# A two-layer graph network on one core: new start and end of the instruction order, adjacency casts behind the weights, row sums of the first attention on TensorE

## The chip, the cores and the metric

One core of one Trainium2 chip runs the kernel in one launch. The metric is the device time of that core in microseconds. The engines named below are TensorE (PE; its weight loads are shown apart as PEld), VectorE (DVE), ScalarE (ACT), GpSimd (POOL) and SyncE (SP). SP computes nothing here; it issues transfers.

## The reference

32 graphs of 512 nodes with 256 features each go through two layers. Heads are 8 with 32 features. Shortened:

```python
def layer0(x, adj):                       # transformer layer
    allowed = (adj > 0) | (adj.T > 0) | eye
    q, k, v = split(x @ Wqkv.T + bqkv)
    attn = softmax(where(allowed, (q / sqrt(32)) @ k.T, -inf))
    x = layernorm(x + (attn @ v) @ Wo.T + bo) * g1 + b1n
    return layernorm(x + relu(x @ W1.T + b1) @ W2.T + b2) * g2 + b2n
def layer1(x, adj):                       # attention alone, mask adj != 0
    return (softmax(where(adj != 0, q @ k.T / sqrt(32), -inf)) @ v) @ Wo.T + bo
x = layernorm(x + layer0(x, adj))
x = layernorm(x + layer1(x, adj))
```

All of it is float32; adj is a 512 x 512 int32 matrix for each graph.

## The kernel before

Each graph is an object (`class Graph`, L218) whose methods issue one step of the work each. All steps are written out by hand in one order: `opening` (L630, the first five graphs until the pattern repeats), `period` (L1534, called for k = 1 to 26, with five neighbouring graphs a to e in different stages), and `closing` (L1837, the last five graphs). Every engine executes its own instructions in exactly that order, and a step waits for its inputs and for the buffer that it writes. Which of several buffers a tile gets is written out too, as strings of digits (`slots`, L166): "d" for the three PSUM banks of the dense products, "p" for the eight buffers of attention weights, and so on.

The steps that matter here, with P = 128, NQ = 4 blocks of nodes, ND = 2 blocks of features:

- `load` (L310) brings x of a graph to SBUF by SP. `constants(a, b)` (L337) issues the loads of entries a to b-1 of a list of weights by SP: 0 is Wqkv (768 KB), 1 to 3 its biases, 4 and 5 Wo and bo of layer 0, 6 and 7 W1 (1 MB) and b1, 8 and 9 W2 and b2, 10 to 13 norm weights, 14 to 21 layer 1, 22 a second copy of b2 as a column.
- `cast` (L313) turns adj into bf16 by a DMA from POOL's queue (HBM to HBM). `entries` (L319) loads the result, `entry(i)` (L322) loads a block of it transposed, both from SP. `masks(i)` (L325) makes the two masks of it on DVE.
- `transpose` and `transpose_out` make xT of the first graph on PE and ACT (tile psT). For later graphs `flip`, `sort` (transfers by SP) and `join` (ACT) do that.
- `query_key` (psQK), `value` (psV), `project` (psO), `hidden` (psH) and `mlp` (psF) are products through `dense` (L159), which issues them with 128 columns of weights (`wide=True`) or four times with 32.
- `scores(layer, k)` (L441) writes 4 heads x 512 scores of a block of 128 keys to the one tile s in PSUM; `exp` (L456) takes it to a p buffer on ACT; `masked` (L459) multiplies p by the mask on DVE; `product` (L463) multiplies p with v on PE into the one tile acc, and `context` copies that out on ACT. Eight values of k make an attention.
- The row sums of p are needed to divide. `pair` (L479) adds one p to another by an accumulating DMA of POOL's queue, `fold` (L483) adds two on DVE. For heads 0 to 3 `halve` (L505) and `spread` (L510) go on by DMA and `blocks` and `reduce` end it on DVE; for heads 4 to 7 `sums` (L486) adds over partitions on PE, 4 products with a matrix of ones (tile psR). Where `direct` (L244) is true, which holds for the last graph's layer 1 only, there is no folding: `sums` runs 16 products for each half of the heads.
- `once(i)` (L342) computes constants on PE: 0 and 1 bv @ Wo (4 matmul instructions each), and 2 the product of W1 with the column b2, whose moving side has one column, 32 matmul instructions. The result is subtracted from b1 in `once_out`.
- `store` (L627) writes the result of a graph by one transfer of SP.

A float32 product appears as two matmul instructions in the trace. The order of the old opening, until the second graph's first product, is:

```python
a.load(); a.cast(); a.constants(0, 4); a.transpose(0, 1); a.transpose_out(0, 1); b.flip(1); b.sort(1, 0, 0)
a.entries(); a.transpose(0, 0); a.transpose_out(0, 0); a.query_key(0, 0, 0, None, wide=True); a.entry(3)
a.entry(1); a.query_key_out(0, 0, 0, None); b.cast(); a.query_key(0, 1, 0, None, wide=True)
a.query_key_out(0, 1, 0, None); a.entry(0); a.entry(2); a.masks(0); a.scores(0, 3); a.exp(0, 3)
a.scores(0, 2); a.exp(0, 2); a.query_key(0, 1, 1, None); b.flip(0); a.scores(0, 0); a.exp(0, 0); a.masks(1)
a.masks(2); a.value(0, 0); a.value_out(0, 0); a.scores(0, 1); b.sort(1, 0, 1); a.exp(0, 1)
a.query_key(0, 0, 1, None); a.query_key_out(0, 1, 1, None); a.query_key_out(0, 0, 1, None); a.value(0, 1)
a.masked(0, 0); b.sort(1, 1, 0); a.value_out(0, 1); a.masked(0, 1); a.scores(0, 5); a.exp(0, 5)
a.constants(22, 23); a.product(0, 0); a.pair(0, 0); a.constants(4, 6); a.once(0); b.sort(0, 1, 0)
a.product(0, 1); b.sort(0, 0, 0); a.masked(0, 2); a.constants(10, 12); a.masked(0, 3); b.sort(1, 1, 1)
a.scores(0, 4); a.exp(0, 4); a.masked(0, 4); a.scores(0, 6); b.sort(0, 1, 1); b.join(0, 1); a.exp(0, 6)
a.product(0, 2); a.scores(0, 7); a.exp(0, 7); a.masked(0, 7); a.product(0, 3); a.context(0, 0); b.join(1, 0)
b.sort(0, 0, 1); a.pair(0, 2); a.fold(0, 2, 2, 0); a.product(0, 4); a.once_out(0); a.bias(1); b.join(0, 0)
b.entry(0); b.value(0, 0); b.join(1, 1); b.query_key(0, 1, 0, None)
...
```

The old closing ends with:

```python
e.product(1, 7); e.guard(0, 0, 1); e.widen(1, 1); e.context(1, 1); e.divide(1, 1); e.project(1, 0)
e.add(4, 1); e.add(4, 0); e.stats(4, 1); e.guard(0, 1, 1); e.guard(1, 0, 0); e.project(1, 1); e.stats(4, 0)
e.aggregate(4, 0); e.aggregate(4, 1); e.add(4, 3); e.add(4, 2); e.stats(4, 3); e.stats(4, 2)
e.aggregate(4, 3); e.aggregate(4, 2); e.root(4, 0, 2); e.offset(4, 0, 2); e.norm(4, 1); e.norm(4, 0)
d.guard(1, 0, 0); e.root(4, 2, 4); e.guard(1, 1, 1); e.offset(4, 2, 4); e.norm(4, 3); e.norm(4, 2)
e.store()
```

Of the kernel before, what the change touches and what calls it, by code (L numbers as in the profile page):

```python
# [14 lines left out]
ALU = mybir.AluOpType  # L15
# [12 lines left out]
def kernel(ctx: ExitStack, tc: tile.TileContext, t: dict, out: bass.AP):  # L28
# [12 lines left out]
    nc = tc.nc  # L41
    x, adj = t["x"], t["adj"]
    B, N, D = x.shape
    P = 128
# [106 lines left out]
    def plain(pools: ExitStack):  # L151
# [7 lines left out]
        def dense(out, lhsT, rhs, start, stop, wide):  # L159

            for at in (slice(0, P),) if wide else [slice(j * HD, (j + 1) * HD) for j in range(HPC)]:
# [3 lines left out]

        slots = {  # L166
            "d": iter(
                "012012021021122121012012010210210210201012102021121021012012012012102102102102102020120122021201212101120120212010"
                + "120121212010121212012012120120021212102101010212101010210210102102201010" * 13
                + "102120201210021021010210102102102021201021010210202101201201210210212102102102121021021021021021202102120120"  # L170
            ),
            "p": iter(
                "012345673267415013405762302764517064153205732146706431520752136450436217051726431"
                + "036472501257436206435710271536470436152075216435036421705172436106437250125736420436571027156437036415207521436506432170517236410436725012576432036457102715436706431520752136450436217051726431" * 2
                + "03642750175246370435612072516437063124563452170"
            ),
            "y": iter(
                "01231023012301231023100113201320232301321023020231201302"
                + "303021031230232301321023020231201302" * 8
                + "3202132031200210203102312020021032101230"  # L180
            ),
            "z": iter(
                "011010010110"
                + "01101001" * 13
                + "011010010101"
            ),
            "st": iter(
                "01230123012301230132103210321032102310231023"
                + "12032103210321031230213021302130" * 13
                + "1203123012031023031203210312031203123210320132013021"  # L190
            ),
            "r": iter(
                "0123331303"
                + "23301003" * 13
                + "11100313021131"
# [7 lines left out]
                "01100110"  # L203
                + "0110" * 13
                + "0110"
            ),
            "total": iter(
                "01110"
                + "0110" * 13
                + "0101001"  # L210
# [7 lines left out]
        class Graph:  # L218
# [25 lines left out]
            def direct(self, layer):  # L244

                return (self.b, layer) == (B - 1, 1)
# [62 lines left out]

            def load(self):  # L310
                nc.sync.dma_start(out=self.x, in_=x[self.b].rearrange("(c p) d -> p c d", p=P))

            def cast(self):  # L313
                nc.gpsimd.dma_start(
                    out=self.code.rearrange("(p c) k -> p (c k)", p=P),
                    in_=adj[self.b].rearrange("(p c) k -> p (c k)", p=P),
                )

# [18 lines left out]
            def constants(self, a, b):  # L337

                for dst, src in resident[a:b]:
                    nc.sync.dma_start(out=dst, in_=src)  # L340

            def once(self, i):  # L342
# [8 lines left out]
                ps = self.bank("B", (i,), [NF])  # L351
                for f in range(NF):
                    for c in range(ND):
                        nc.tensor.matmul(  # L354
                            ps[:, f : f + 1],
                            w1[:, c, f * P : (f + 1) * P],
                            b2_c[:, c : c + 1],
# [4 lines left out]
            def once_out(self, i):  # L362
# [4 lines left out]
                nc.vector.tensor_tensor(b1, b1, self.bank("B", (i,), [NF]), ALU.subtract)  # L367
# [259 lines left out]
            def store(self):  # L627
                nc.sync.dma_start(out=out[self.b].rearrange("(c p) d -> p c d", p=P), in_=self.x2)

        def opening(a, b, c, d, e):  # L630

            a.load()
            a.cast()
            a.constants(0, 4)
            a.transpose(0, 1)
            a.transpose_out(0, 1)
            b.flip(1)
            b.sort(1, 0, 0)
            a.entries()
            a.transpose(0, 0)  # L640
            a.transpose_out(0, 0)
            a.query_key(0, 0, 0, None, wide=True)
            a.entry(3)
            a.entry(1)
            a.query_key_out(0, 0, 0, None)
            b.cast()
            a.query_key(0, 1, 0, None, wide=True)
            a.query_key_out(0, 1, 0, None)
            a.entry(0)
            a.entry(2)  # L650
            a.masks(0)
            a.scores(0, 3)
            a.exp(0, 3)
            a.scores(0, 2)
            a.exp(0, 2)
            a.query_key(0, 1, 1, None)
            b.flip(0)
            a.scores(0, 0)
            a.exp(0, 0)
            a.masks(1)  # L660
            a.masks(2)
            a.value(0, 0)
            a.value_out(0, 0)
            a.scores(0, 1)
            b.sort(1, 0, 1)
            a.exp(0, 1)
            a.query_key(0, 0, 1, None)
            a.query_key_out(0, 1, 1, None)
            a.query_key_out(0, 0, 1, None)
            a.value(0, 1)  # L670
            a.masked(0, 0)
            b.sort(1, 1, 0)
            a.value_out(0, 1)
            a.masked(0, 1)
            a.scores(0, 5)
            a.exp(0, 5)
            a.constants(22, 23)
            a.product(0, 0)
            a.pair(0, 0)
            a.constants(4, 6)  # L680
            a.once(0)
            b.sort(0, 1, 0)
            a.product(0, 1)
            b.sort(0, 0, 0)
            a.masked(0, 2)
            a.constants(10, 12)
            a.masked(0, 3)
            b.sort(1, 1, 1)
            a.scores(0, 4)
            a.exp(0, 4)  # L690
            a.masked(0, 4)
            a.scores(0, 6)
            b.sort(0, 1, 1)
            b.join(0, 1)
            a.exp(0, 6)
            a.product(0, 2)
            a.scores(0, 7)
            a.exp(0, 7)
            a.masked(0, 7)
            a.product(0, 3)  # L700
            a.context(0, 0)
            b.join(1, 0)
            b.sort(0, 0, 1)
            a.pair(0, 2)
            a.fold(0, 2, 2, 0)
            a.product(0, 4)
            a.once_out(0)
            a.bias(1)
            b.join(0, 0)
            b.entry(0)  # L710
            b.value(0, 0)
            b.join(1, 1)
            b.query_key(0, 1, 0, None)
            a.halve(0, 0, P // 2)
            b.query_key(0, 0, 0, None)
            b.query_key_out(0, 0, 0, None)
            b.query_key_out(0, 1, 0, None)
            b.query_key(0, 1, 1, None)
            b.scores(0, 0)
            b.value(0, 1)  # L720
            a.halve(0, 0, P // 4)
            b.exp(0, 0)
            a.masked(0, 5)
            a.product(0, 5)
            b.value_out(0, 1)
            b.query_key(0, 0, 1, None)
            a.masked(0, 6)
            b.scores(0, 2)
            a.fold(0, 3, 6, 7)
            a.product(0, 6)  # L730
            a.product(0, 7)
            a.pair(0, 4)
            b.exp(0, 2)
            a.fold(0, 3, 3, 4)
            a.constants(20, 22)
            b.query_key_out(0, 1, 1, None)
            a.constants(6, 8)
            a.spread(0, 0, 0)
            b.query_key_out(0, 0, 1, None)
            b.scores(0, 3)  # L740
            a.spread(0, 0, 1)
            b.exp(0, 3)
            a.spread(0, 0, 3)
            a.spread(0, 0, 2)
            b.entry(2)
            a.blocks(0, 0)
            a.reduce(0, 0)
            b.scores(0, 7)
            b.exp(0, 7)
            a.constants(17, 20)  # L750
            a.sums(0, 1)
            a.blocks(0, 1)
            a.invert(0, 1)
            a.once(2)
# [2196 lines left out]
```

## Time and profile before

| | |
|---|---|
| median of 3 runs | 2998.94 us (2998.46 to 3000.49) |
| the profiled execution | 2999.72 us |
| its span, first to last instruction | 2998.0 us |
| PE busy | 2959.6 us |
| DVE, ACT, POOL busy | 2707.0, 1747.1, 978.6 us |
| one period (the same product of successive graphs, 385.91 and 477.49 us) | 91.6 us |
| first matmul | 4.93 us |
| last matmul of the last graph ends | 2986.4 us |
| last store issued | 2991.1 us |

The busy time of PE says how long some matmul was in flight, not how fast: a matmul at half clock counts as busy for twice as long. The record of the granted clock starts only at about 22 us (before that it reads 1.00 whatever the durations are), so the clock of the first 20 us is read from durations. In lists in order of time, each line has start and length in us, engine, source line, operation, output <- inputs, shape and number of instructions, and in brackets how long the engine stood idle before it and what ended that.

### The profile page before, as it was taken

The numbers are of one execution on the slowest core, as the hardware profiler recorded it, in microseconds if no ns is written. First come the engines' busy times: TensorE is split into PE (matmuls) and PEld (weight loads), VectorE is DVE, ScalarE is ACT, GpSimd is POOL, SyncE is SP. The second block draws the span as 40 slices with busy tenths as digits, with TensorE's granted clock in tenths as the row PEclk, the third lists the DMA queues.
The fourth block names the chain that finished last, engine by engine and source line by source line (L and its number), as shares of the span: only waits on it lengthen the run. The fifth ranks groups of instructions, "written<-read, shape, count | busy, mean of one in ns | idle before, by whom it ended". The sixth has DMA issues, their size and how long they took to land.

```text
span 2998.0 us, 83024 instructions
## 1 busy us (share of the span) xinstructions
PE 2959.6 (99%) x36442; PEld 1374.8 (46%) x36442; DVE 2707.0 (90%) x3588; ACT 1747.1 (58%) x2111; POOL 978.6 (33%) x1252
## 2 busy tenths in 40 slices
PE   7999999999999999999999999999999999999997
PEld 2544444544444544445444445444454444554443
DVE  4899999999999999999999999999999999999996
ACT  4455656556655566555566555665555665556654
POOL 0222333323333233333233332333332333323241
PEclk9999999999999999999999999999999999999999
DMA  6776766767667676666676676766666776667560
GB/s 155 139 138 121 152 132 134 130 131 143 135 126 136 128 147 125 134 133 130 130 144 132 128 137 129 145 126 133 134 129 131 145 133 126 137 128 142 101 114 27
DMA packets 277169, 391.22 MB, mean 130 GB/s; under 512 B 153376, under 2 KB 237472, under 8 KB 246048
## 3 DMA queue, kind: packets, MB, share of 16 engines
q0 software_dynamic: 36304, 264.53, 47.8%
q1 hardware_dynamic: 240496, 121.32, 18.1%
q8 instruction: 288, 4.72, 0.6%
q14 instruction: 81, 0.66, 0.1%
HBM read 72.23 MB, written 33.55 MB: 35 GB/s over the span
## 4 chain that ended last, share of the span: by engine, by line
PE 95%; DVE 2%; DMA 1%; ACT 1%; POOL 0%; issue 0%; SPq 0%; DVEq 0%; POOLq 0%; ACTq 0%
PE s L448 17%; PE psH L162 15%; PE psF L162 15%; PE acc L468 15%; PE psQK_None L162 11%; PE psO L162 7%; PE psV L162 7%; PE psQK L162 4%; PE psT L409 2%; PE psR L492 2%; DVE p L461 1%; ACT p L457 1%; DVE p L484 1%; DMA p<-p 1%; DMA w_L_gnn_Wqkv<-in_L_gnn_Wqkv_dram 0%; PE psB L354 0%
## 5 line engine op out<-in xcount | busy, mean ns | idle before, releaser
L457 ACT ACTIVATE p<-s 128x2048 f32<-128x2048 f32 x512 | 963.4, 1882 | 488.6 <-PE s L448 482.8
L461 DVE TENSOR_TENSOR p<-p,m 128x2048 f32<-128x2048 f32 x512 | 1162.3, 2278 | 39.2 <-ACT p L457 36.3
L448 PE MATMUL s<-qT,kT 32*64 32x512 f32 x8192 | 570.7, 613 | 10.8 <-ACT p L457 9.5
L468 PE MATMUL acc<-p,v 128*32 128x512 f32 x4096 | 507.6, 595 | 1.6 <-ACT cT L477 1.5
L162 PE MATMUL psH<-xT,w_L_gnn_W 128*32 128x256 f32 (+1 forms) x6200 | 470.8, 380 | 0.0
L162 PE MATMUL psF<-w_L_gnn_W,hT 128*32 128x256 f32 (+1 forms) x6704 | 459.8, 379 | 0.0
L484 DVE TENSOR_TENSOR p<-p,p 128x2048 f32<-128x2048 f32 x189 | 431.0, 2281 | 10.3 <-DMA p<-p 9.0
L583 POOL TENSOR_SCALAR rs<-mv 128x2 f32<-128x2 f32 (+1 forms) x320 | 198.4, 620 | 708.8 <-DVE mv L578 693.6
L162 PEld LDWEIGHTS psH<-xT,w_L_gnn_W 128*32 128x32 f32 (+1 forms) x6200 | 302.1, 118 | 197.8 <-issue 55.3
L584 POOL TENSOR_TENSOR rs<-rs,neg_half 128x2 f32<-128x2 f32 (+1 forms) x320 | 372.2, 1163 | 26.7
L162 PEld LDWEIGHTS psF<-w_L_gnn_W,hT 128*32 128x32 f32 (+1 forms) x6704 | 290.3, 116 | 179.5 <-ACT hT L619 32.6
L481 POOL DMA_DIRECT2D p<-p x189 | 174.8, 925 | 531.5 <-PE acc L468 462.3
L619 ACT ACTIVATE hT<-psH,c_L_gnn_b 128x256 f32<-128x256 f32 x512 | 211.7, 474 | 195.4 <-PE psH L162 195.4
L448 PEld LDWEIGHTS s<-qT,kT 32*64 32x64 f32 x8192 | 119.2, 129 | 323.9 <-issue 114.0
L508 POOL DMA_DIRECT2D p<-p x126 | 107.7, 855 | 464.4 <-DVE mv L578 202.4
L162 PE MATMUL psQK_None<-xT,w_L_gnn_Wqkv 128*32 128x512 f32 (+1 forms) x2012 | 247.2, 599 | 6.0 <-DMA w_L_gnn_Wqkv<-in_L_gnn_Wqkv_dram 4.7
L162 PE MATMUL psO<-w_L_gnn_Wo,cT 128*32 128x256 f32 (+1 forms) x2776 | 241.7, 381 | 1.2 <-DVE cT L554 1.2
L468 PEld LDWEIGHTS acc<-p,v 128*32 128x32 f32 x4096 | 119.5, 109 | 253.2 <-issue 188.1
L162 PEld LDWEIGHTS psO<-w_L_gnn_Wo,cT 128*32 128x32 f32 (+1 forms) x2776 | 155.0, 123 | 98.1 <-issue 43.8
L414 ACT COPY xT<-psT 128x512 f32<-128x512 f32 x130 | 76.1, 585 | 199.3 <-PE psT L409 199.1
L604 ACT ACTIVATE x<-z,ms,rs 128x256 f32<-128x256 f32 x128 | 73.1, 597 | 166.2 <-DVE ms L588 163.0
L575 DVE BATCH_NORM_STATS2 st<-y 128x6 f32<-128x256 f32 x384 | 155.0, 422 | 6.2
(77 smaller groups left out, 2849.8 us busy)
## 6 DMA issues: line engine op xcount, KB each, us to landing
p<-p POOLq DMA_DIRECT2D x189, 1024.0 KB, 7.9
p<-p POOLq DMA_DIRECT2D x63, 512.0 KB, 5.9
x<-in_x_dram SPq DMA_DIRECT2D x32, 512.0 KB, 4.2
code<-in_adj_dram POOLq DMA_DIRECT2D x32, 512.0 KB, 5.9
m<-code SPq DMA_DIRECT2D x32, 512.0 KB, 4.9
out_dram<-x SPq DMA_DIRECT2D x32, 512.0 KB, 6.2
p<-p POOLq DMA_DIRECT2D x63, 256.0 KB, 5.9
part<-p SPq DMA_DIRECT2D x252, 64.0 KB, 2.0
```

The costliest lines, as they stand in the source:

```text
L162: nc.tensor.matmul(out[at], lhsT[:, at], rhs, start=start, stop=stop)
L448: nc.tensor.matmul(s[half * P // 2 : (half + 1) * P // 2, j, :], self.kT(layer)[at, hg, key : key + P // 2], self.qT(layer)[at, hg, :], st ...
L457: nc.scalar.activation(self.p(layer, k), self.at("s", (layer, k), [HPC, N]), AF.Exp, scale=SCALE)
L461: nc.vector.tensor_tensor(p, p, m[:, k % NQ, None, :].to_broadcast([P, HPC, N]), ALU.mult)
L468: nc.tensor.matmul(acc[j * HD : (j + 1) * HD, :], self.v(layer)[:, kc, h * HD : (h + 1) * HD], self.p(layer, k)[:, j, :], start=(kc == 0), ...
L481: nc.gpsimd.dma_start(out=self.p(layer, k), in_=self.p(layer, k + 1), accum_op=ALU.add)
L484: nc.vector.tensor_tensor(self.p(layer, dst), self.p(layer, a), self.p(layer, b), ALU.add)
L508: nc.gpsimd.dma_start(out=p[:rows], in_=p[rows : 2 * rows], accum_op=ALU.add)
L575: nc.vector.bn_stats(self.at("st", (n, i), [6]), self.y(n, i))
L583: nc.gpsimd.tensor_scalar(rs, self.mv(n)[:, a:b, 1:2], EPS, None, ALU.add)
L584: nc.gpsimd.tensor_tensor(rs, rs, neg_half[:, a:b, None], ALU.pow)
L619: nc.scalar.activation(self.hT(h)[:, f, :], ps[:, f % 2, :], AF.Relu, bias=b1[:, f : f + 1])
```

## The change

- The cast of the first graph gets a wait for the load of Wqkv, that of the second graph for the load of W1.
- `warm` issues four products of 512 columns on a constant ahead of the first transposes.
- The attention of layer 0 of the first graph becomes `direct`: its row sums are made by 2 x 16 products on PE; its three `pair`, three `fold`, two `halve` and four `spread` calls go.
- `once(2)` streams 64 equal columns in place of one, in a full PSUM bank, and is called earlier.
- `store` can write half; the last graph's result goes out in two halves.
- `opening` and `closing` have a new order. `period` is unchanged, call by call; its buffers rotate in a new order (new strings in `slots`, with x and xT now listed as well).

```diff
+        first = {}
...
             def direct(self, layer):
 
-                return (self.b, layer) == (B - 1, 1)
+                return (self.b, layer) in ((0, 0), (B - 1, 1))
...
+            def warm(self):
+
+                ps = self.bank("W", (0,), [N])
+                for _ in range(4):
+                    nc.tensor.matmul(
+                        ps,
+                        ones[:, 0:1].to_broadcast([P, P]),
+                        ones[:, 0:1].to_broadcast([P, N]),
+                        start=True,
+                        stop=True,
+                    )
+
             def load(self):
                 nc.sync.dma_start(out=self.x, in_=x[self.b].rearrange("(c p) d -> p c d", p=P))
 
-            def cast(self):
-                nc.gpsimd.dma_start(
+            def cast(self, behind=None):
+                code = nc.gpsimd.dma_start(
                     out=self.code.rearrange("(p c) k -> p (c k)", p=P),
                     in_=adj[self.b].rearrange("(p c) k -> p (c k)", p=P),
                 )
+                if behind is not None:
+                    wait = mybir.DependencyInfo(mybir.DependencyClass.Sync, mybir.DependencyReason.SCHED_ONLY)
+                    tc.add_manual_dep(code.ins, behind.ins.name, wait, reason="weights first")
...
             def constants(self, a, b):
 
-                for dst, src in resident[a:b]:
-                    nc.sync.dma_start(out=dst, in_=src)
+                loads = [nc.sync.dma_start(out=dst, in_=src) for dst, src in resident[a:b]]
+                first[a] = loads[0]
...
-                ps = self.bank("B", (i,), [NF])
+                ps = self.bank("B", (i,), [NF, P // 2])
                 for f in range(NF):
                     for c in range(ND):
                         nc.tensor.matmul(
-                            ps[:, f : f + 1],
+                            ps[:, f, :],
                             w1[:, c, f * P : (f + 1) * P],
-                            b2_c[:, c : c + 1],
+                            b2_c[:, c : c + 1].to_broadcast([P, P // 2]),
                             start=(c == 0),
                             stop=(c == ND - 1),
...
-                nc.vector.tensor_tensor(b1, b1, self.bank("B", (i,), [NF]), ALU.subtract)
+                nc.vector.tensor_tensor(b1, b1, self.bank("B", (i,), [NF, P // 2])[:, :, 0], ALU.subtract)
...
-            def store(self):
-                nc.sync.dma_start(out=out[self.b].rearrange("(c p) d -> p c d", p=P), in_=self.x2)
+            def store(self, half=None):
+                at = slice(0, NQ) if half is None else slice(half * NQ // 2, (half + 1) * NQ // 2)
+                nc.sync.dma_start(out=out[self.b].rearrange("(c p) d -> p c d", p=P)[:, at, :], in_=self.x2[:, at, :])
```

The new opening, until the first hidden layer:

```python
a.load(); a.constants(0, 4); a.warm(); b.flip(1); a.transpose(0, 0); a.transpose(0, 1)
a.transpose_out(0, 0); a.cast(first[0]); a.constants(22, 23); a.transpose_out(0, 1)
a.query_key(0, 1, 0, None, wide=True); a.query_key(0, 0, 0, None, wide=True); a.query_key_out(0, 1, 0, None)
a.query_key_out(0, 0, 0, None); a.scores(0, 2); a.exp(0, 2); a.entries(); a.value(0, 1); a.scores(0, 1)
a.exp(0, 1); a.query_key(0, 0, 1, None); a.query_key_out(0, 0, 1, None); a.entry(2); a.scores(0, 0)
a.entry(0); a.exp(0, 0); a.entry(1); a.value(0, 0); a.entry(3); a.constants(6, 8); b.cast(first[6])
a.value_out(0, 0); b.sort(1, 0, 0); a.masks(0); a.masks(1); a.scores(0, 3); a.query_key(0, 1, 1, None)
a.masks(2); a.masked(0, 0); b.flip(0); a.masked(0, 2); a.constants(4, 6); b.sort(1, 0, 1); a.masked(0, 1)
b.sort(1, 1, 0); a.exp(0, 3); a.masked(0, 3); a.query_key_out(0, 1, 1, None); a.scores(0, 4)
b.sort(0, 0, 0); a.value_out(0, 1); a.exp(0, 4); a.masked(0, 4); b.sort(0, 1, 0); a.scores(0, 5)
a.exp(0, 5); a.once(2); a.scores(0, 6); b.sort(0, 1, 1); a.masked(0, 5); a.exp(0, 6); a.product(0, 0)
a.product(0, 1); a.product(0, 2); a.scores(0, 7); b.sort(1, 1, 1); a.exp(0, 7); b.sort(0, 0, 1)
b.join(0, 0); a.product(0, 3); a.sums(0, 0); a.once(0); b.entries(); b.join(1, 0); a.context(0, 0)
b.entry(1); b.join(0, 1); a.product(0, 4); a.constants(12, 14); a.masked(0, 6); a.product(0, 5)
a.masked(0, 7); a.constants(20, 22); a.product(0, 6); a.product(0, 7); a.blocks(0, 0); a.reduce(0, 0)
a.constants(8, 10); a.sums(0, 1); a.constants(17, 20); a.once_out(0); a.context(0, 1); a.bias(1)
b.join(1, 1); b.query_key(0, 1, 0, None); a.blocks(0, 1); a.guard(0, 1, 0); b.query_key(0, 0, 0, None)
b.load(); b.entry(3); c.flip(1); b.query_key_out(0, 1, 0, None); a.invert(0, 1); a.widen(0, 1)
a.divide(0, 1); b.value(0, 0); b.query_key_out(0, 0, 0, None); a.invert(0, 0); a.widen(0, 0); b.entry(2)
b.scores(0, 0); a.divide(0, 0); b.value_out(0, 0); a.project(0, 0); a.project(0, 1); b.exp(0, 0)
b.scores(0, 1); a.add(1, 1); a.stats(1, 1); a.add(1, 0); c.cast(); a.stats(1, 0); a.aggregate(1, 1)
a.add(1, 3); a.aggregate(1, 0); a.once(1); a.constants(10, 12); b.exp(0, 1); a.center(1, 1); a.once_out(2)
a.stats(1, 3); b.query_key(0, 1, 1, None, wide=True); a.masks(3); a.root(1, 0, 2); a.add(1, 2)
a.stats(1, 2); a.affine(1, 1); a.center(1, 0); a.affine(1, 0); b.query_key(0, 0, 1, None, wide=True)
a.aggregate(1, 2); b.query_key_out(0, 1, 1, None); a.transpose(1, 0); b.entry(0); b.masks(0)
a.aggregate(1, 3); a.center(1, 3); b.query_key_out(0, 0, 1, None); a.transpose_out(1, 0); a.root(1, 2, 4)
b.scores(0, 2); a.hidden(0, 2)
...
```

The new closing ends with:

```python
e.product(1, 7); e.context(1, 1); e.divide(1, 1); d.norm(4, 2); e.project(1, 1); e.bias(2); e.project(1, 0)
e.add(4, 2); e.add(4, 3); e.stats(4, 3); e.stats(4, 2); e.aggregate(4, 3); e.aggregate(4, 2)
e.root(4, 2, 4); e.guard(1, 1, 1); d.norm(4, 3); e.add(4, 1); e.add(4, 0); d.guard(1, 0, 0); e.stats(4, 1)
d.store(); e.stats(4, 0); e.aggregate(4, 1); e.aggregate(4, 0); e.offset(4, 2, 4); e.norm(4, 2)
e.root(4, 0, 2); e.offset(4, 0, 2); e.norm(4, 3); e.store(1); e.norm(4, 1); e.guard(0, 0, 1); e.norm(4, 0)
e.store(0)
```

## The prediction

> **What bounds the kernel now.** I read the page's busy shares first, then the busy time by stretch of time, then the instructions in order of time for the first 90 us and the last 30, then the waits of TensorE. The page:
>
> ```profile
> PE 2959.6 (99%) x36442; PEld 1374.8 (46%) x36442; DVE 2707.0 (90%) x3588; ACT 1747.1 (58%) x2111; POOL 978.6 (33%) x1252
> PE   7999999999999999999999999999999999999997
> ```
>
> TensorE (PE) is the bound: only 2998.0 - 2959.6 = 38.4 us of the span are without a matmul, and they lie in the first and the last slice. The stretches of time say so exactly (length, then busy us of PE, its weight loads, DVE, ACT, POOL, then granted clock and DMA):
>
> ```profile
> 0.00:10.00 10.00, 1.94 (x8) 1.57 (x8) 0.23 (x1) 2.46 (x3) 2.09 (x11) 1.00 0.86 236
> 10.00:20.00 10.00, 6.60 (x24) 2.38 (x24) 0.00 (x0) 2.32 (x3) 0.00 (x0) 1.00 0.64 134
> 70.00:80.00 10.00, 9.74 (x49) 7.33 (x42) 6.17 (x10) 2.84 (x3) 0.79 (x2) 0.50 1.00 181
> 100.00:400.00 300.00, 300.00 (x4000) 137.91 (x3996) 274.36 (x359) 169.31 (x208) 91.20 (x122) 1.00 0.70 132
> 400.00:1000.00 600.00, 600.00 (x7252) 278.94 (x7244) 555.68 (x734) 361.52 (x437) 207.11 (x258) 1.00 0.69 134
> 2850.00:2980.00 130.00, 125.56 (x1712) 54.69 (x1708) 111.18 (x168) 67.40 (x85) 41.91 (x61) 1.00 0.37 71
> 2990.00:2998.00 8.00, 0.00 (x0) 0.00 (x0) 0.10 (x1) 0.57 (x2) 0.00 (x0) 0.60 0.26 76
> ```
>
> From 90 to 2850 us PE never pauses. The period's calls are the same before and after, so nothing can be won or lost there unless new slots make a wait. Idle in the ten stretches up to 90 us sums to 21.6 us. The rest of the start's loss is hidden in the durations, in order of time:
>
> ```profile
> 4.93 1.94 PE L409 MATMUL psT<-ident,x 128*128 128x128 f32 x8 [4.93 <-DMA x<-in_x_dram]
> 11.58 5.48 PE L162 MATMUL psQK_None<-xT,w_L_gnn_Wqkv 128*128 128x512 f32 x8 [4.70 <-DMA w_L_gnn_Wqkv<-in_L_gnn_Wqkv_dram]
> 22.04 3.60 PE L162 MATMUL psQK_None<-xT,w_L_gnn_Wqkv 128*32 128x512 f32 x16
> 29.77 1.92 PE L162 MATMUL psQK_None<-xT,w_L_gnn_Wqkv 128*32 128x512 f32 x16
> 71.00 1.94 PE L492 MATMUL psR<-p,ones 128*32 128x512 f32 x8 [0.26 <-DVE p L484]
> 72.87 6.99 PE L354 MATMUL psB<-c_L_gnn_b,w_L_gnn_W 128*128 128x1 f32 x32
> 79.72 3.76 PE L162 MATMUL psO<-w_L_gnn_Wo,cT 128*128 128x256 f32 x8
> ```
>
> The same product takes 3.60 us at 22 us and 1.92 at 30 us: at 22 us PE runs at half clock. Half clock costs 0.9 (transposes, against 2 x 0.5 later), 2.0 (first Q and K, 5.48 against 8 x 0.43), 1.7 (at 22 us), 0.4 (the scores at 69 us, 1.51 against 1.11), 0.9 (sums), 1.9 (projection, 3.76 against 1.89), and 3.1 in W1's column product (6.99 against an estimate of 3.9: 32 x 0.12, the spacing of the 128-column transposes at full clock). Together 10.9. **Loss at the start before: 21.6 + 10.9 = 32.5 us.** The waits name the two largest gaps, and the DMA view the transfers behind them (KB, median us to landing):
>
> ```profile
> PE psT L409 <- DMA x<-in_x_dram: 4.9, 1, 4.9
> PE psQK_None L162 <- DMA w_L_gnn_Wqkv<-in_L_gnn_Wqkv_dram: 4.7, 1, 4.7
> w_L_gnn_Wqkv<-in_L_gnn_Wqkv_dram SPq DMA_DIRECT2D x1, 768.0 KB, 10.2
> x<-in_x_dram SPq DMA_DIRECT2D x1, 512.0 KB, 4.1
> ```
>
> **What the Trainium skill says.** "TensorE: Matmul & The Clock Gate", Part 1: the clock is half by default, full after about 3.4 us of sustained matmuls, half again after an idle window of that length, and the window runs free of the kernel. The trace agrees: QK turned fast 3.6 us after 11.58, and both later drops (22.0 and 69.8 us) end a stretch of 3.4 us in which PE was busy 40%; a stretch with 50% (45.9 to 49.3) did not drop, one with 81% (69.8 to 73.2) did not raise it. The 6.99 us of one-column products, busy throughout, did not raise it either. "DMA: Bandwidth & Descriptors", Issuing engines are not separate DMA queues: transfers from all issuers share the same 16 engines and interleave. The trace agrees: Wqkv needed 10.2 us while two adjacency casts, issued at 1.38 and 2.48 us, ran; x, ahead of most of them, needed 4.1.
>
> **The change part by part.**
>
> *Casts behind weights.* Bytes until Wqkv landed: x 0.5, Wqkv 0.8, casts 1.05 written (twice that read) MB. Without the casts Wqkv follows x directly. x lands at about 4.4; Wqkv's 768 KB at the 421 GB/s of the stretch from 4 to 5 us take 1.9 us, plus under 1 us of completion: 7.0 us (bounds 6.4 and 11.4, no gain). That is no longer what QK waits for, see the next step. The wait sits on POOL; behind the first cast there is only the second cast (which waits for W1), and then a guard needed at about 55 us: no cost. The mask path moves: cast issued at 7.1, landed at 13 (5.9 us, the page's median), then entries and four transposes on SP (4 x 1.27) and 3.7 us of landing: masks at 21.5, as before (21.84). Behind entries SP holds W1: issued about 19, landed at 26 (7.1 us); it is needed at 31.
>
> *Warm matmuls.* Four float32 products of 512 columns are eight instructions like QK's eight: 0.86 us each at half clock, 0.43 at full. They start at about 1.2 us. The clock rises at the end of the first window that is full, between 4.5 and 7.9 us by its free phase; so they end between 6.3 and 8.0, taken as 7.1. x has landed at 4.4: they delay the transposes by 2.7 us, more than they need to. Transposes at full clock (2 x 0.5) to 8.1, ACT's copies (0.59 each, the second at 8.3) to 8.9: **QK starts at 9.0** instead of 11.58, Wqkv having 2 us of cover, and runs at full clock, 3.45 us (bounds: 8.2 with an early clock, 11.5 if Wqkv doesn't profit; QK up to 5.5 us if the clock is not up).
>
> *Sums of graph 0, layer 0 on PE.* 16 products (32 instructions) take 3.46 us (sums of the last graph: 2971.22 to the next at 2974.68). Added: 2 x 3.46 - 0.86 = 6.1 us on PE. Removed: three folds (3 x 2.28 on DVE), three pairs, two halves, four spreads. Their DMA chain (7.0 and 9.6 us on the chain of waits at 43 and 59 us) is why PE stands idle between 40 and 70; all of that idle time goes. What is late next: DVE's eight masked products, from 21.5 + 2.35 on, 8 x 2.28: done by 42 to 47 us; PE reaches the last product at about 52. Hidden, with some 5 us of cover.
>
> *New order at the start.* I followed the new list call by call, each engine in its own order, with these durations; the same walk over the old list puts the first hidden layer at 88.8, the trace at 89.4. PE time without useful work left after: 8.0 (to 9.0, less 1.0 of transposes; the warm matmuls are in it), 0.8 (first qT), 3 x 0.18 (scores behind exp), 0.9 and 2.0 (scores 4 and 5 at 26 to 31 us, behind ACT), 0.5 (near 115 us). Sum 12.7. With the sums (6.1): 18.8 us. Gain if the clock then holds: 32.5 - 18.8 = 13.7.
>
> *W1's column product.* It moves from 73 us to right behind the weak spot: between 26.0 and 31.2 us PE has just two score groups, 2.2 us of work in 5.2. Nearly every phase of the window finds 3.4 us there with 40% or less, as at 22.0 and 69.8 us. So I expect half clock from 29 to 32 us on. With 64 columns the product streams about half of each 0.216 us slot, which the 81% stretch says is too little to raise the clock; it takes 7.0 again (3.1 lost; bounds 0 and 5), and the dense work behind it runs 3.4 to 6.8 us more at half speed, 2.6 lost on average. Gain 13.7 - 5.7 = 8.0.
>
> *Closing.* Same PE work. The old closing is idle 5.4 us between 2850 and 2984; the walk gives the new order 2.8 us more, and since it overstates the old one by 2.4 times, I take 1.2 worse (bounds -1 and +3). From the last matmul to the last norm both take about 4.1 to 4.8 us. The last store was issued at 2991.1 and moved data for about 2.4 us; half of it in advance saves 1.0 (0 to 1.5). Net 0.2 worse.
>
> **Sum.** Gain 7.8 us. Span 2998.0 - 7.8 = 2990.2; 1.7 us lie around it (2999.72 for the profiled execution); the median of the runs shown, 2998.94, is 0.8 below that one: **2991.1 us**.
>
> **Rivals.** (1) The clock holds through 26 to 31 us, because the phase falls well or because streaming 64 columns counts as activity: nothing lost to half clock there, gain 13.5, 2985.4. For it: a 50% stretch held before. Against: 40% dropped twice. (2) The casts' wait doesn't free the weights (it doesn't reach the issue, or graph 1's transposing load takes the casts' place): Wqkv at 11.4, QK 2.5 later, gain 5.3, 2993.6. Against: that load stands behind Wqkv in SP's queue. (3) Slower: the clock drops at 29 us and does not return, because small waits keep every window below full. Each us at half clock costs half a us; the 13.7, less 3.1 in the column product and 0.2, are eaten after 2 x 10.4 = 21 us of it beyond that product. If it holds until 76 us, 38 us beyond the product, the change loses 8.6 and ends near 3007.5. Against: from 38 us on the walk shows no waits on PE.
>
> **How the numbers follow.** Forecast 0.54 (own range 2987.5 to 2994), rival 1 0.26, rival 2 0.15, rival 3 0.05. The range 2984 to 2995.5 takes in the first three but for their outer ends. 0.2% is 6.0 us, about what a measurement of this kernel can tell from no change. Over 6 us faster: eight tenths of the forecast, all of rival 1 and a third of rival 2, 0.43 + 0.26 + 0.05 = 0.74; slower: 0.04, most of rival 3; within: the rest, 0.22.
>
> **What would show it.** QK's first product starts near 9.0 with eight matmuls in 3.5 us; masks start near 21.5; PE shows no wait for DMA p<-p before 60 us; the column product at about 31 us takes 7 us (forecast) or 4 (rival 1), with 0.50 or 1.00 as the clock; the first hidden layer starts near 76 us or 70; the period stays 91.6 us. Wrong would be: a wait of PE for W1 or for masked p, any idle PE time in the middle, or a closing that loses more than 3 us.

## The result and the profile after

The changed kernel takes **2994.88 us** in the median of 22 runs (2992.98 to 3003.18), the one before 2998.43 in 22 runs beside it. The ratio of the means is 0.999, with an interval of 0.9984 to 0.9997: some 3 us are gained, 3.6 by the medians, where 7.8 were forecast, and the gain is less than the 0.2% that the prediction named as the limit of what counts as faster. The profiled execution took 2996.1 us, its span is 2994.3 (before: 2999.72 and 2998.0).

First the line of busy shares, as shown of before:

```profile
PE 2968.1 (99%) x36842; PEld 1371.5 (46%) x36842; DVE 2700.5 (90%) x3585; ACT 1747.3 (58%) x2111; POOL 998.8 (33%) x1247
```

PE is busy 8.5 us longer than before, so its idle time fell from 38.4 to 26.2 us. But 12.2 us less idle time made the span only 3.7 us shorter: busy time is not useful time here. The busy time by stretch says where it went (length, busy us of PE, weight loads, DVE, ACT, POOL, then granted clock and DMA):

```profile
25.28:28.69 3.41, 1.12 (x16) 0.24 (x16) 3.41 (x3) 2.61 (x3) 0.52 (x1) 1.00 1.44 276
30.00:40.00 10.00, 10.00 (x64) 7.23 (x48) 7.04 (x4) 1.88 (x1) 0.00 (x0) 0.50 0.60 163
2850.00:2980.00 130.00, 122.85 (x1660) 53.20 (x1656) 106.80 (x159) 65.46 (x80) 38.52 (x57) 0.99 0.37 70
```

From 400 to 1000 us PE is as full as before (600.00 us busy of 600.00). From 30 to 40 us PE is full too, but at half clock; the stretch just ahead of it, 25.28 to 28.69, has 1.12 us of matmul in 3.41. And the stretch from 2850 to 2980 lost 2.7 us of PE time (before: 125.56), with a clock of 0.99 in the mean. In order of time, the start:

```profile
1.09 5.54 PE L326 MATMUL psW<-ones 128*128 128x512 f32 x8 [1.09 <-POOL total L66]
...
8.23 3.70 PE L162 MATMUL psQK_None<-xT,w_L_gnn_Wqkv 128*128 128x512 f32 x8 [0.73 <-ACT xT L441]
...
29.10 2.02 PE L475 MATMUL s<-qT,kT 32*64 32x512 f32 x16 [2.03 <-ACT p L484]
31.04 7.09 PE L381 MATMUL psB<-c_L_gnn_b,w_L_gnn_W 128*128 128x64 f32 x32
...
45.80 3.62 PE L519 MATMUL psR<-p,ones 128*32 128x512 f32 x32
```

Query and key start at 8.2 us instead of 11.6 and run at full clock. The DMA view has the reason (KB, median us to landing):

```profile
w_L_gnn_Wqkv<-in_L_gnn_Wqkv_dram SPq DMA_DIRECT2D x1, 768.0 KB, 5.7
```

Wqkv needs 5.7 us instead of 10.2. All waits of PE for a DMA are gone from the first 90 us. Then comes the weak spot of the new order: the scores at 29.10 wait 2.03 us for exp, and from 28.7 to 42.3 us the clock is half. W1's column product takes 7.09 us (before, also at half clock: 6.99). Behind 42.3 us PE doesn't wait until 100 us, and the first hidden layer starts at 74.2 us instead of 89.4.

Two differences tell the start from the end. I take the 251st exp of the run, near 1460 us, as a mark in the middle: it starts 7.47 us earlier than before. The last instruction comes 3.7 us earlier. **The opening won 7.5 us, and the closing gave 3.8 of it back.** PE in order of time near the end, first before, then after:

```profile
2939.03 0.65 PE L409 MATMUL psT<-ident,x 128*128 128x128 f32 x4
2940.36 1.13 PE L162 MATMUL psQK<-xT,w_L_gnn_Wk 128*128 128x256 f32 x4 [0.68 <-ACT xT L414]
2941.32 1.03 PE L162 MATMUL psQK<-xT,w_L_gnn_Wq 128*128 128x256 f32 x4
...
2948.11 1.11 PE L448 MATMUL s<-qT,kT 32*64 32x512 f32 x16
...
2951.26 1.12 PE L448 MATMUL s<-qT,kT 32*64 32x512 f32 x16 [0.18 <-ACT p L457]
```

```profile
2932.46 0.66 PE L436 MATMUL psT<-ident,x 128*128 128x128 f32 x4
...
2938.12 0.33 PE L436 MATMUL psT<-ident,x 128*128 128x128 f32 x1 [0.61 <-ACT qT L465]
2938.88 0.55 PE L436 MATMUL psT<-ident,x 128*128 128x128 f32 x3 [0.43 <-ACT x L631]
2940.10 1.92 PE L162 MATMUL psQK<-xT,w_L_gnn_Wk 128*128 128x256 f32 x4 [0.67 <-ACT xT L441]
2941.81 1.91 PE L162 MATMUL psQK<-xT,w_L_gnn_Wq 128*128 128x256 f32 x4
2944.29 1.12 PE L475 MATMUL s<-qT,kT 32*64 32x512 f32 x16 [0.56 <-ACT qT L465]
...
2947.80 1.12 PE L475 MATMUL s<-qT,kT 32*64 32x512 f32 x16 [1.40 <-ACT kT L465]
```

From the first of these transposes to the last graph's first scores the old order needs 9.1 us, the new one 11.8 us. Of the 2.7 more, 1.7 are half clock: the two products at 2940 take 1.92 and 1.91 us, in the old order 1.13 and 1.03. The rest has two parts. The waits of PE in this stretch sum to 2.3 us instead of 1.9, with waits for qT, for x and again for qT that the old order doesn't have; and the lines left out hold a value product of 1.89 us, where the old order has one more query or key product. The next scores come 3.51 us later instead of 3.15, after a wait of 1.40 us for kT, whose copy stands behind an exp of 1.88 us on ACT.

### The profile page after: what moved, and what is told of

Read it like the earlier page. It is cut to its first block, busy times and chain, and to the rows that moved or that the text cites. A ratio compares the mean times of both kernels' runs of the same rounds, so it can differ in the third digit from the quotient of the medians.

```text
span 2994.3 us, 83802 instructions
## 1 busy us (share of the span) xinstructions
PE 2968.1 (99%) x36842; PEld 1371.5 (46%) x36842; DVE 2700.5 (90%) x3585; ACT 1747.3 (58%) x2111; POOL 998.8 (33%) x1247
## 3 DMA queue, kind: packets, MB, share of 16 engines
q8 instruction: 291, 4.77, 0.6%
## 4 chain that ended last, share of the span: by engine, by line
PE 96%; DVE 2%; ACT 1%; DMA 0%; issue 0%; POOL 0%; SPq 0%; DVEq 0%; POOLq 0%
PE s L475 18%; PE acc L495 15%; PE psH L162 15%; PE psF L162 14%; PE psQK_None L162 11%; PE psV L162 7%; PE psO L162 7%; PE psQK L162 4%; PE psT L436 2%; PE psR L519 2%; ACT p L484 1%; DMA p<-p 0%; DVE p L488 0%; DVE st L602 0%; PE psB L381 0%
## 5 line engine op out<-in xcount | busy, mean ns | idle before, releaser
L610 POOL TENSOR_SCALAR rs<-mv 128x2 f32<-128x2 f32 (+1 forms) x320 | 210.9, 659 | 686.6 <-DVE mv L605 668.1
L511 DVE TENSOR_TENSOR p<-p,p 128x2048 f32<-128x2048 f32 x186 | 424.1, 2281 | 4.2 <-DMA p<-p 3.0
```

The source lines that it names most:

```text
L511: nc.vector.tensor_tensor(self.p(layer, dst), self.p(layer, a), self.p(layer, b), ALU.add)
L610: nc.gpsimd.tensor_scalar(rs, self.mv(n)[:, a:b, 1:2], EPS, None, ALU.add)
```

## The experiments

My theory: the opening is right as forecast and is limited by the half clock that the gap at 26 to 31 us sets off; the closing's order loses what is missing. Rivals: the loss at the end is the last graph's own latency, whatever the order; or the narrow product, the warm matmuls or the casts' wait act otherwise than forecast. Twelve kernels were run. The kernel before was timed beside all of them, with medians of 2998.4 to 2999.8, so each kernel also has its ratio to the runs beside it. This is a ratio of means, which a few long runs pull up: after has two, of 3003.18 and 3000.97 us, and old_opening_new_closing, whose runs spread from 2998.05 to 3019.0, has two over 3012. Medians don't feel them. "Lead" is that of the 251st exp, "end" that of the span's end, both in one profile, against the profile of before. A lead hangs in part on when the clock first rises, which differs from profile to profile: with the same four warm products it rose at 4.3 to 7.1 us, and query and key, where they didn't wait for Wqkv, started at 8.0 to 9.4 us.

| kernel | median us | ratio to before, interval | lead | end | given back |
|---|---|---|---|---|---|
| after | 2994.88 | 0.9990 (0.9984 to 0.9997) | 7.5 | 3.7 | 3.8 |
| new_opening_old_closing | 2992.03 | 0.9977 (0.9968 to 0.9986) | 7.3 | 7.9 | -0.6 |
| old_opening_new_closing | 3002.89 | 1.0018 (1.0008 to 1.0027) | -1.4 | -5.0 | 3.6 |
| fill_opening_gap | 2988.42 | 0.9964 (0.9951 to 0.9976) | 12.6 | 11.3 | 1.3 |
| fill_closing_gaps | 2994.52 | 0.9986 (0.9980 to 0.9993) | 7.9 | 5.6 | 2.3 |
| fill_and_old_closing | 2986.22 | 0.9958 (0.9944 to 0.9971) | 13.4 | 14.0 | -0.6 |
| no_cast_wait | 2996.78 | 0.9992 (0.9985 to 0.9999) | 3.7 | 1.4 | 2.3 |
| one_column | 2994.47 | 0.9984 (0.9978 to 0.9991) | 6.3 | 4.7 | 1.6 |
| no_warm | 2995.29 | 0.9986 (0.9979 to 0.9992) | 0.5 | -2.3 | 2.8 |
| base_no_warm | 2986.78 | 0.9959 (0.9946 to 0.9973) | 12.9 | 13.5 | -0.6 |
| base_short_warm | 2984.34 | 0.9951 (0.9937 to 0.9964) | 15.0 | 15.6 | -0.6 |
| base_fewer_sums | 2982.41 | 0.9944 (0.9930 to 0.9958) | 16.6 | 16.2 | 0.4 |
| base_halved_store | 2986.19 | 0.9957 (0.9943 to 0.9971) | 13.4 | 13.6 | -0.2 |

**Opening and closing apart.** The edits exchange the list of `closing`, with the digits in `slots` mapped so that every buffer follows the one that it followed before.

```diff
-            d.guard(1, 0, 0)
-            e.stats(4, 1)
-            d.store()
...
-            e.store(1)
-            e.norm(4, 1)
-            e.guard(0, 0, 1)
-            e.norm(4, 0)
-            e.store(0)
+            e.norm(4, 3)
+            e.norm(4, 2)
+            e.store()
```

> The opening of after with the closing of before (its buffers renamed to match). Theory (the opening gains 7.5 us and the new closing gives 3.7 to 4.0 of it back): 2991.0 us, 7.4 us under before and 3.8 under after, with no clock drop in the last 60 us. Rival (the lead is lost at the end whatever the closing's order, because the last graph's chain is bound by its own latencies): 2994.9, the same as after.

> The opening of before with the closing of after (its buffers renamed to match). Theory (the closing's order alone costs 3.7 to 4.0 us, half of it idle TensorE and half one stretch of half clock): 3002.3 us, 3.9 above before. Rival (the new closing is no worse, and something that the new opening leaves behind slows it): 2998.4, the same as before.

Measured: 2992.03 and 3002.89. The new opening with the old closing is 2.9 us faster than the change as a whole by medians, 3.9 by ratios, and its lead of 7.3 us is still there at the end (7.9). The new closing behind the old opening is 3.5 us slower than before (5.4 by ratios) and gives 3.6 us back in its profile. The theory holds on both sides, and the rivals fall: the loss belongs to the closing's order and needs nothing of the new opening. Its size is less sure: 2.9 to 3.5 us by medians, and the 5.4 rests on the long runs.

**The gap at 29 us.**

```diff
             a.scores(0, 4)
...
+            a.fill("B", (2,), [NF, P // 2], 512, 2)
             a.scores(0, 5)
```

`fill` issues two products of `warm`'s kind into the bank that the column product uses next.

> After, with two float32 products of 512 columns on constants ahead of the scores of block 5 of graph 0, which now wait 2.03 us for exp. They take 0.86 us each at full clock. Theory (the half clock from 28.7 to 42.3 us is set off by the thin stretch before it): no half clock there, W1's column product about 3.9 us instead of 7.1, and 2989.4 us, 5.5 under after. Rival (the narrow products of 64 columns themselves make the clock fall, or it falls anyway in that stage): half clock remains, 2994.9 or 1 to 2 more.

Measured: 2988.42, one us better than expected. PE in order of time:

```profile
28.12 1.99 PE L339 MATMUL psB<-ones 128*128 128x512 f32 x4
30.22 1.12 PE L488 MATMUL s<-qT,kT 32*64 32x512 f32 x16
31.27 3.79 PE L394 MATMUL psB<-c_L_gnn_b,w_L_gnn_W 128*128 128x64 f32 x32
```

The fillers fit into the wait, the scores start no later behind them, and the column product takes 3.79 us instead of 7.09. The clock stays full to the end of the work. By the medians this is worth 6.5 us. The lead grows by 5.2 us only, but in this profile the clock also rose 2.3 us later at the start; with the old closing, the same fillers (fill_and_old_closing against new_opening_old_closing) win 6.1 us of lead and 5.8 us by medians. The half clock costs some 6 us. Work that computes nothing, laid into a wait, is worth more than the whole change was.

**The closing with its gaps filled.**

```diff
+            e.fill("T", (2, 1), [ND, 2 * P], 256, 1)
             e.transpose(2, 1)
             e.transpose_out(2, 1)
+            e.fill("QK", (1, 1, 0, 1), [2 * P], 256, 1)
```

> After, with one product of 256 columns on constants (0.43 us) ahead of the transposes of the last graph's second half, which wait 0.61 us, and one more after them, where query and key wait 0.67 us for the copy. Theory (about 1.7 us of the closing's loss is the half clock that this thin stretch sets off): no half clock at 2940, 2993.0 us, 1.9 under after. Rival (the loss is the order's own waits, and the fillers delay the work behind them): 2994.9 to 2995.8.

Measured: 2994.52, between the two. In its profile the half clock is gone:

```profile
2931.72 0.66 PE L449 MATMUL psT<-ident,x 128*128 128x128 f32 x4
...
2937.37 0.70 PE L339 MATMUL psT<-ones 128*128 128x256 f32 x2 [0.61 <-ACT qT L478]
...
2939.34 0.70 PE L339 MATMUL psQK<-ones 128*128 128x256 f32 x2 [0.68 <-ACT xT L454]
2939.88 1.02 PE L162 MATMUL psQK<-xT,w_L_gnn_Wk 128*128 128x256 f32 x4
```

The two products (the second, of 1.03 us, follows at 2940.74) take 2.05 us together instead of 3.83, but the waits still stand and the fillers, 0.70 us long, add some 0.5 us of their own: from the transposes ahead to query and key it is 8.2 us instead of 7.6. Given back are 2.3 us instead of 3.8. The times don't separate it from after (0.9986 and 0.9990, intervals overlapping). The table says why the gain is small: four profiles with the new closing, as it is, had no half clock in it (fill_opening_gap, one_column, no_cast_wait, no_warm), and they gave back 1.3 to 2.8 us. Only after and old_opening_new_closing had it, with 3.8 and 3.6. no_cast_wait has the waits of after to within 0.01 us (0.61, 0.43, 0.68, 0.56 and 1.40), and its two products take 1.13 and 1.03 us. So the waits are there in every profile, and the half clock, 1.7 us, comes on top in some. In how many of the runs without a profile it came, their times don't tell.

**Both remedies.** The edits of fill_opening_gap and new_opening_old_closing are made together.

> The opening of after with the two filling products, and the closing of before. Theory (the opening's lead of 12.6 us is kept whole by the closing of before, which gave nothing back behind the new opening): 2986.0 us, 2.4 under the filled kernel and 9 under after. Rival (with the clock held, the closing of after costs nothing that counts): 2988.4, the same as the filled kernel.

Measured: 2986.22, as the theory had it. Its spread is 0.8 us, so I took it as the base for the last experiments.

**The casts' wait.**

```diff
-            a.cast(first[0])
+            a.cast()
...
-            b.cast(first[6])
+            b.cast()
```

> After, with the adjacency casts issued without waiting for weights. Theory (the wait clears the way for the first weights): Wqkv lands at 10 us instead of 7, the first query and key products start at 10 to 11.5 instead of 8.2, scores of graph 0 follow, and the lead at 600 us shrinks from 7.4 to about 4: 2998 us, 3 above after. Rival (the masks of graph 0 are what ends last in the opening, and an earlier cast brings them earlier): masks at 18 us instead of 21, 2994.9 or less.

Measured: 2996.78, 1.9 us above after, and a lead of 3.7 instead of 7.5:

```profile
11.56 5.34 PE L162 MATMUL psQK_None<-xT,w_L_gnn_Wqkv 128*128 128x512 f32 x8 [4.12 <-DMA w_L_gnn_Wqkv<-in_L_gnn_Wqkv_dram]
```

PE waits 4.12 us for Wqkv, the clock won by the warm matmuls is lost in that wait (5.34 us instead of 3.70), and the scores that wait for exp come at 34.06 us instead of 29.10. The masks come at 18.9 us instead of 21.2 and bring nothing, as the scores set the pace. So the wait on POOL's queue earns half of the opening's gain by the lead, 3.7 us; by the medians it earns 1.9. The 21 runs spread from 2990.86 to 3001.67. The four fastest, 2990.86 to 2993.84, have a mean clock of 0.998 or 0.999, the others 0.997 or less, so part of what the wait earns hangs on whether the clock falls.

**The 64 columns.**

```diff
-                ps = self.bank("B", (i,), [NF, P // 2])
+                ps = self.bank("B", (i,), [NF])
...
-                            ps[:, f, :],
+                            ps[:, f : f + 1],
...
-                            b2_c[:, c : c + 1].to_broadcast([P, P // 2]),
+                            b2_c[:, c : c + 1],
```

> After, with W1's column product streaming one column again, at its new place. Theory (what it costs is its weight loads, and 64 columns neither slow it nor hold the clock): 7.0 us at half clock as with 64 columns, 2994.9 us, within 0.5 of after. Rival (streaming 64 columns keeps the clock up or shortens the half clock): half clock lasts longer or comes again, 2996.5 to 2999.

Measured: 2994.47, and 6.99 us for the product instead of 7.09, half clock for 13.65 us in both. From the start of query and key to the first sums it is 37.7 us, with 64 columns 37.6. (The lead is 1.2 us smaller because the clock first rose at 6.87 us instead of 4.83, and query and key started at 9.25.) Streaming 64 columns does nothing that shows; the product is bound by its 32 weight loads, which in after fill the whole of the window from 32.10 to 35.51 us (3.41 of 3.41).

**The warm matmuls.** Twice without them, and once with half of them.

```diff
-            a.warm()
```

> After without the four products on constants ahead of x. Theory (they only lift the clock for the first transposes and the first query and key products, some 7 us of work at the start, the rest of which waits for the adjacency chain anyway): the first stage runs at half clock until about 11 us, the masks still come at 21.2 us, and the whole is 2995 to 2996.5 us, 0 to 1.5 above after. Rival (the warm-up carries a large part of the gain): 2998 us, 3 above after.

Measured: 2995.29, within the theory. The profiled execution was an unlucky one: at 331 us PE waited 4.77 us for a divide, behind which DVE had waited 5.96 us for the transfers of `spread`; no other profile shows this, and half clock followed. So its lead near 1460 us says nothing; until 318 us it was 0.6 us ahead of after. I repeated the experiment on the quieter base.

> The filled opening with the closing of before (2986.2 us), without the four products ahead of x. Theory (what they win in clock they lose again by holding back the transposes, x having landed at 4.9 us and they ending at 6.6 to 7.0): transposes from 4.9 us at half clock, query and key from about 7.5 in 5.2 us, scores some 0.5 us later: 2986.7. Rival (they carry part of the gain, because the clock comes up too late without them): 2988.5 or more.

```diff
-                for _ in range(4):
+                for _ in range(2):
```

> The same filled kernel (2986.2 us), with two products ahead of x in place of four. Theory (two are done by 4.6 us, before x lands, and the clock comes up all the same): transposes from about 5.0 us, query and key from 7.0 to 7.5, held by Wqkv, in 3.5 to 4.5 us: 2985.2, 1.0 faster. Rival (the gap between them and x keeps the clock down): query and key in 5.2 us, 2986.7.

Measured: 2986.78 without, 2984.34 with two products, against 2986.22 with four. With two:

```profile
1.09 3.54 PE L326 MATMUL psW<-ones 128*128 128x512 f32 x4 [1.09 <-POOL total L66]
4.88 1.06 PE L449 MATMUL psT<-ident,x 128*128 128x128 f32 x8 [0.25 <-DMA x<-in_x_dram]
7.03 3.67 PE L162 MATMUL psQK_None<-xT,w_L_gnn_Wqkv 128*128 128x512 f32 x8 [1.08 <-DMA w_L_gnn_Wqkv<-in_L_gnn_Wqkv_dram]
```

They end as x lands, the clock is up, and query and key wait for Wqkv alone. What four products win, 0.6 us, is not clear of the spread (2985.76 to 2986.53 with them, 2986.28 to 2987.82 without), and after against no_warm, 0.4 us by medians, isn't either. Two products win 2.4 us (2984.17 to 2984.61), because the other two hold the transposes back. This version beats the kernel before by 0.49% (0.9937 to 0.9964) and is the best that I have.

**The direct sums.**

```diff
-                folded = [2 + hg] if not self.direct(layer) else range(hg * NQ, (hg + 1) * NQ)
+                folded = [2 + hg] if not self.direct(layer) else range(hg * NQ, hg * NQ + (1 if self.b == 0 else NQ))
```

> The same filled kernel (2986.2 us); graph 0's row sums of layer 0 take in only the first of four blocks of keys, so 24 of 32 products are left out. Theory (the direct sums lie wholly on TensorE's path and hide nothing): 0.75 x 7.24 = 5.4 us less, 2980.8. Rival (DVE's masked products are what the next products wait for, and the sums only fill that time): 2984 to 2986.

Measured: 2982.41, 3.8 us less, between the two but nearer to the theory. Its lines:

```profile
40.28 1.04 PE L532 MATMUL psR<-p,ones 128*32 128x512 f32 x8
...
43.22 3.64 PE L508 MATMUL acc<-p,v 128*32 128x512 f32 x32 [0.84 <-ACT cT L517]
...
48.22 3.64 PE L162 MATMUL psQK_None<-xT,w_L_gnn_Wqkv 128*32 128x512 f32 x32 [0.50 <-ACT xT L439]
```

2 x 2.58 us of sums go, and two new waits, 0.84 for the copy of the context and 0.50 for xT, take 1.3 of it back. What is late next behind the sums is ACT, not DVE's masked products.

**The store in halves.**

```diff
             e.norm(4, 0)
+            e.store(0)
...
-            e.store()
+            e.store(1)
```

> The same filled kernel (2986.2 us), with the last graph's result stored in two halves, the first as soon as its two blocks are normed. Theory (most of the time after the last issue is fixed, whatever the size): 0.3 us less, 2985.9. The forecast's step: 1.0 less, 2985.2.

Measured: 2986.19, nothing gained. The whole store was issued at 2977.53 us and landed 4.2 us later, the second half at 2977.90 and 3.7 us later: 2981.7 and 2981.6 us. In after and before the same pair is 3.9 and 4.4 us. The Trainium skill, "DMA: Bandwidth & Descriptors", Anatomy of one DMA, gives about 2 us of a transfer (there one of GpSimd's path) as fixed and the rest by size. Its rate gives an estimate of 0.6 us for 256 KB less, and the 0.5 us measured agree; but the first half, as large as the second, landed 2.1 us after its issue, so a fixed part and a size don't explain the 3.7. Beside the second half, and not beside the first, the two queues that the profile calls instruction moved 80 KB. Whether these held it up was not tried.

## Why the prediction was right and where it failed

- **Casts behind weights: right.** Forecast: QK at 9.0 instead of 11.5, 2.5 us. Measured: 8.2 against 11.6 without the wait, and 1.6 us of clock beside, lost in the wait of 4.12 us. By the medians the step is worth 1.9 us, by the lead 3.7. The 8.2 is in part luck, an early rise of the clock, within the stated bounds. The masks came at 21.2 us, forecast 21.5. Nothing queued behind the wait on POOL was missed.
- **Warm matmuls: right on the clock and on the delay.** "More than they need to" was borne out: all four together win 0.4 to 0.6 us by medians, not clear of the spread, and two of them alone 2.4.
- **Sums on PE: right.** No wait for DMA in the stage. All but 1.3 us of what 24 products take lie on the path, as the forecast charged them. What the old chain would have cost behind the new order was not run.
- **W1's column product: right.** Half clock from 28.7 us, forecast 29 to 32; 7.09 us, forecast 7.0; cost 5.2 to 6.1 us by leads and 5.8 to 6.5 by medians, forecast 5.7. One reading in this step was wrong: the stretch from 69.8 to 73.2 us of before, read as 81% busy, has matmuls in 92% of its time (3.15 of 3.41 us, with the start of the column product). That the product wouldn't raise the clock came true all the same. Rival 1, a clock that holds, didn't come by itself; when forced it gave leads of 12.6 and 13.4, the rival's gain was 13.5.
- **The opening's sum: right,** 7.5 us against 8.0. Other profiles of the same opening give leads of 7.3 and 7.9, and the runs with the old closing are 7.3 us under before by medians.
- **The closing: this step failed.** The prediction wrote "I take 1.2 worse (bounds -1 and +3) ... Net 0.2 worse". Measured are 3.8 us in the profile, beyond the 3 us that it named as what would prove it wrong; by runs, 2.9 (3.9 by ratios) behind the new opening, which is just under 3, and 3.5 (5.4) behind the old. My walk had given the new order 2.8 us more, and I scaled it down since it overstated the old order's idle time by 2.4 times. That was the error: an idle sum that is too large for both orders doesn't make their difference too large. Idle PE time from 2680 us to the last matmul is 5.4 us before and 7.3 after, 1.9 worse, where I took 1.2; in the other profiles with the new closing as it is, it is 7.5 to 8.0. The second part was missing altogether: I priced the clock at every weak spot of the opening and at none of the closing, where a fall of the clock costs 1.7 us in two of the profiles. The third, "half of it in advance saves 1.0", is 0.2 to 0 us: 0.5 us are saved in the transfer, but the last half is issued later, 4.9 us after the last matmul instead of 4.7. Of the 3.8 us 0.4 stay unplaced.

So 7.8 was forecast and some 3 to 3.6 came. The measured 2994.88 lies outside the range that the prediction gave its own forecast (2987.5 to 2994) and inside the wider one that takes in the rivals (2984 to 2995.5) by 0.6 us. The outcome that it held likeliest, over 6 us faster at 0.74, didn't come. That it still fell in there is luck, since the terms of the closing had not foreseen its loss. Rival 2 came nearest with 2993.6 us, but its reason didn't hold: Wqkv did profit, and landed in 5.7 us instead of 10.2. Not tried: the new opening with the old chain of accumulating transfers, and a closing that puts single waits right one at a time; which of the new waits costs how much is read from the trace and not shown by a run.

## What to carry to other kernels

Where TensorE is the bound, look for the thinnest 3.4 us of each stage and price the clock there, at the end of the kernel as well as at its start; a few products on constants, sized to fit a wait that is there anyway, paid more here than the whole new order. Matmuls that warm the clock did best here when they ended as the data landed; those beyond that delayed the work that they were meant to help. And when a model of two orders is wrong on the one that is known, take its difference with wider bounds, not scaled down.

## What the runs showed of the hardware

The Trainium skill, "TensorE: Matmul & The Clock Gate", HAM oscillation, tells of drops behind idle gaps of over 3.4 us. Here no such gap is needed: the longest wait in the stretch at 25.3 to 28.7 us is 2.03 us. In every profile, the changes of the clock lie whole multiples of 3.413 us apart, so I cut each profile into windows of this length on its own edges. (The record starts with the first rise of the clock, at 15.2 us before, not at 22, and at 4.3 to 16.6 us in the others.) A window at full clock that had matmuls in 0.40 of its time or less was followed by half clock every time: 12 such windows lie in the openings and the middle, 14 at the very end of the work. A window with 0.53 or more was never followed by a drop. At 0.46 to 0.51 it went both ways: of seven such windows two dropped, both at 0.50 with 0.87 to 0.88 us of transposes among their 1.7 us (2936.9 to 2940.3 us in after is one).

The same page, PE-mode transpose, says that a transpose doesn't count as busy in the same way. The two windows would fit that, but others show that transposes here do not count for nothing: a window at 4.27 us in base_short_warm had 0.61 with its transposes and 0.30 without, one at 2940.2 us in no_cast_wait 0.63 and 0.37, and the clock held after both. What sets the two apart is open.

Once half, the clock stayed half for 10.2 to 13.65 us where the column product followed soon, though PE was full, and for 3.41 us where products of 256 or 512 columns followed at once (at 2940 us in after, at 11.5 us in no_cast_wait).
